# Two recurrent blocks in one launch: the layers of the first block in another order, one transpose used twice, four buffers for routed results, and longer runs at the end

## The chip, the cores and the metric

The kernel runs on one core of one Trainium2 chip. A core has five engines that run side by side, each through its own list of instructions in order: TensorE (PE; its weight loads are listed apart as PEld), VectorE (DVE), ScalarE (ACT), GpSimd (POOL) and SyncE (SP), which issues most of the transfers. Transfers run on 16 DMA engines. The metric is the device time of one execution in microseconds (us); lower is better.

## The reference, cut to what matters

The input is 32 sequences of 256 tokens, 128 numbers each (8192 tokens). There are two blocks of the form `x = x + s * silu(f)`, where `s` is a mixer and `f` a mixture of experts, both fed by the same layer norm of `x`.

```python
# block 0
xn = layernorm(x)
s = transformer(xn)          # 2 layers; layer 0 begins with layernorm(xn) * g + b
f = moe64(xn)                # 64 experts, top 8, 64 slots each, plus a shared expert
x = x + s * silu(f)
# block 1
xn = layernorm(x)
s = linear_attention(xn)
f = moe32(xn)                # 32 experts, top 1, plus a shared expert
x = x + s * silu(f)
```

What matters below: layer 0 of the transformer norms `xn`, which is a layer norm already. The second norm of a normed row is the same row times one number, the *ratio* of that token. So the router and the shared expert read `xn`, and the attention projection reads `xn` times the ratio of each token.

## The kernel before, in words

**Tiles.** Tokens are worked on in 16 groups of 512 (`g`), four tiles of 128 tokens each. Rows with a token on each partition are kept on the chip for the whole run (`s_rows`, also `s_all`). Matrix products need the other form, a channel on each partition, so rows are transposed on TensorE (four 128x128 transposes into one bank of `ps_tr`, of which there are two) and copied out by ScalarE. Groups go in pairs `p` = 0 to 7; a pair in one layer is a unit, so block 0's transformer has 16 units.

**Block 0.** In step `k` of a loop over units, `softmax` does the attention of unit `k`. Beside it `beside(k)` does the second norm, the first half (`widen`, L733) and second half (`narrow`, L748) of the feed-forward part of earlier units, and then `project` (L624, L634) for unit `k + 1`. The order of the units is written out by hand (`order_of`, L594): (0,0), (1,0), (2,0), (0,1), (3,0), (1,1), (4,0), (2,1) and so on, pair first, layer second. Layer 1 of a pair comes three or four units after its layer 0.

`enter(g)` loads `x`, takes its statistics on VectorE (L411, L412), and computes `xn` on POOL (L432); it stores `xn` to a table in DRAM, transposes it and keeps the transposed form `xs` (five buffers, `lent[g]`) for `choose` (router, L450) and `shared` (shared expert, L489 to L501). `norm_t(g)` makes the input of `project`. In layer 0 it takes `z` = `xn` * ratio on POOL (L608, four instructions), transposes it (L152, four) and copies it (L612) to `xt`; groups 0 and 1 have their `z` from `enter`. In layer 1, and for the feed-forward part, it norms `s_rows` first (L129 to L145).

In every second step `search` looks for the tokens of each expert on VectorE (L508, L509, 1024 elements wide), a quarter of the tokens at a time; each quarter ends with three fills of zeros in DRAM, together some 4.1 MB, issued by SP. When all quarters are found, `experts` gathers rows (L548), multiplies (L562, L574), scales the result into `e_y` (L584, ScalarE) and adds it to `sums` in DRAM with an indirect transfer issued by POOL (L585). `e_y` and `s_y`, the result of the shared expert (L500), share two buffers (tag "y").

**Block 1.** `route` (router, shared expert `shared1`, whose result goes to `back` in DRAM), `send` (scatters rows by expert), `linear_attention`, `routed` (expert tiles; results are added to `back` by an indirect transfer, L1070), and `finish`, which loads `back` (L1110), takes its silu (L1111, ScalarE), multiplies and adds (L1113, L1114, VectorE) and stores the output (L1115). A column of `s_rows`, `numbers`, says to which row of `back` each token's result goes. A group lies in `back` in the order of the tokens: on a partition stand two tokens that follow each other, and then two others, so a transfer has runs of 1 KB.

**Order.** The instructions are not run in the order of the program. `arrange` takes all of them, a cost for each and what each needs, and writes down one order for every engine (a list schedule, forward and backward passes). The loops above thus set what may run beside what, and `arrange` sets where each instruction stands. All buffers are a part of what it knows.

Of the kernel before, what the change touches and what calls it, by code (L numbers as in the profile page):

```python
# [18 lines left out]
F32 = mybir.dt.float32  # L19
# [8 lines left out]
P = 128  # L28
# [38 lines left out]
def recurrent_kernel(ctx: ExitStack, tc: tile.TileContext, x, consts, small0, wsd, wgu, wd, small1, bias1, wr, out):  # L67
# [24 lines left out]
    xslot = dram.tile([S1 * P, D + 2], F32, name="xslot")  # L92
    back = dram.tile([T + S1 * P, D], F32, name="back")

    def rows(ap, g):
        return ap[g * GW : (g + 1) * GW].rearrange("(b p j) d -> p b (j d)", p=P, j=2)

    def halves(ap, g):
        return ap[g * GW : (g + 1) * GW].rearrange("(b p j) d -> p b j d", p=P, j=2)

    def merged(tile_):
        return tile_.rearrange("p (b j) d -> p b (j d)", j=2)
# [1 line left out]

    s_rows = keep.tile([P, NT, D + 2], F32, name="s_rows")
    s_all = s_rows[:, :, :D]
    numbers = s_rows[:, :, D].rearrange("p (b j) -> p b j", j=2)
    pool.iota(numbers, [[SEQ, BATCH], [1, 2]], base=1, channel_multiplier=2, allow_small_or_imprecise_dtypes=True)
    cc, n_cc = columns(CONSTS)
    con = keep.tile([P, n_cc], F32, name="con")  # L110

# [154 lines left out]
    def shared1(g, inner=False):  # L266

        wk = works[0] if g < EARLY else work(g)
        xt = xt_at[g]
        hs = wk.tile([P, 2, GW], F32, tag="wide", name="f_h", bufs=1)  # L270
        for c in range(2):
            gp, up = bank("sc", 4), bank("sc", 4)
            pe.matmul(gp, par1("sg", c * P, P), xt, start=True, stop=True)
            pe.matmul(up, par1("su", c * P, P), xt, start=True, stop=True)
            if not inner and g < TANH:
                act.activation(hs[:, c], gp, AF.Tanh, scale=0.5)
                vec.scalar_tensor_tensor(hs[:, c], hs[:, c], 1.0, gp, ALU.add, ALU.mult)
            else:
                act.activation(hs[:, c], gp, AF.Silu)
            vec.tensor_tensor(hs[:, c], hs[:, c], up, ALU.mult)  # L280
            yield
        ps = bank()
        for j in range(GT):
            for c in range(2):
                pe.matmul(  # L285
                    ps[:, j * D : (j + 1) * D], hs[:, c, j * P : (j + 1) * P], par1("sd", c * D, D),
                    start=c == 0, stop=c == 1,
                )
        ys = wk.tile([P, GT, D], F32, tag="out", name="f_y")
        act.activation(ys, ps.rearrange("p (t d) -> p t d", d=D), AF.Copy, scale=0.5 if not inner and g < TANH else 1.0)  # L290
        sp.dma_start(rows(back, g), merged(ys))
        yield

    def run(*steps):
# [30 lines left out]
    with ExitStack() as c0:  # L325
# [72 lines left out]
        pool.iota(ciota, [[1, C0]], base=0, channel_multiplier=0, allow_small_or_imprecise_dtypes=True)  # L398
        cand = wf.tile([P, NG // 4, C0], F32, name="cand", bufs=1)
        keys, lent, found, twice = {}, {}, [], {}  # L400
        ratio = w0.tile([P, NG, GT], F32, name="ratio")

        def enter(g):

# [14 lines left out]
            if g < 2:  # L419
                for a, b in ((3, 4), (2, 5)):  # L420
                    pool.tensor_tensor(rs[:, a], rs[:, a - 2], power, ALU.pow)
                    vec.tensor_tensor(rs[:, b], mv[:, :, 0], rs[:, a], ALU.mult)
                twice[g] = wk.tile([P, GT, D], F32, name="z", bufs=4)
                for dst, a, b in ((twice[g], 3, 4), (xn, 2, 5)):
                    for j in range(GT):
                        vec.tensor_scalar(dst[:, j], xi[:, j], rs[:, a, j : j + 1], rs[:, b, j : j + 1], ALU.mult, ALU.subtract)
            else:
                pool.tensor_scalar(rs[:, 4], mv[:, :, 0], -1.0, 0.0, ALU.mult, ALU.add)
                pool.tensor_tensor(rs[:, 0], rs[:, 0], rs[:, 2], ALU.mult)
                pool.tensor_tensor(ratio[:, g], rs[:, 0], rs[:, 3], ALU.mult)  # L430
                for j in range(GT):
                    pool.tensor_scalar(xn[:, j], xi[:, j], rs[:, 4, j : j + 1], rs[:, 2, j : j + 1], ALU.add, ALU.mult)  # L432
            yield
# [51 lines left out]
        def shared(g):  # L485
# [10 lines left out]
            yp = bank()  # L496
            for j in range(GT):
                pe.matmul(yp[:, j * D : (j + 1) * D], hs[:, j * P : (j + 1) * P], sd, start=True, stop=True)
            ys = wk.tile([P, GT, D], F32, tag="y", name="s_y")
            act.copy(ys, yp.rearrange("p (t d) -> p t d", d=D))  # L500
            sp.dma_start(rows(moe0[0], g), merged(ys))  # L501
            yield
# [37 lines left out]
        def experts(q):  # L540
# [35 lines left out]
                    start=True, stop=True,  # L576
                )
            yield
            ye = wk.tile([P, 2, D], F32, tag="y", name="e_y")
            for h in range(2):  # L580
                for u in range(2):
                    at = slice(u * C0, (u + 1) * C0)
# [8 lines left out]

        order_of = [(0, 0), (1, 0), (2, 0), (0, 1)]  # L594
        for p in range(3, NG // 2):
            order_of += [(p, 0), (p - 2, 1)]
        order_of += [(p, 1) for p in range(NG // 2 - 2, NG // 2)]

        def norm_t(g, copy, again=True):

            xs = s_all[:, g * GT : (g + 1) * GT]
            z = twice.pop(g, None) if not again else None
            if z is None:
                z = wk.tile([P, GT, D], F32, name="z", bufs=4)
                if again:
                    normed(wk, xs, z)
                for j in range(0 if again else GT):
                    pool.tensor_scalar(z[:, j], xs[:, j], ratio[:, g, j : j + 1], 0.0, ALU.mult, ALU.add)  # L608
            yield
            ps = transposed(z)  # L610
            xt = wk.tile([P, GW], F32, tag="xt", name="xt", bufs=4)
# [494 lines left out]
    def finish(g):  # L1106

        tl = slice(g * GT, (g + 1) * GT)
        gr = xt_at[g].rearrange("p (t d) -> p t d", d=D)
        ins = sp.dma_start(merged(gr), rows(back, g))  # L1110
        act.activation(gr, gr, AF.Silu)  # L1111
        yield
        vec.tensor_tensor(gr, gr, s_all[:, tl], ALU.mult)  # L1113
# [379 lines left out]
```

## Time and profile before

| | |
|---|---|
| median of 3 runs | 1182.28 us (1179.81 to 1184.58) |
| profiled execution | 1182.8 us, of which its span is 1181.0 us |
| mean granted TensorE clock | 0.977 |
| busy: PE, PEld, DVE, ACT, POOL | 92%, 70%, 69%, 63%, 53% |
| DMA | 124.84 MB, mean 106 GB/s |

The span runs from the first to the last instruction; 1.8 us lie around it. In a row of the groups of instructions, the numbers after the count are the time in which any instruction of the group ran, the mean duration of one in ns, and the idle time of the engine just before them with what ended it. Matrix instructions overlap, so a mean duration is longer than the step from one to the next. In the trace a float32 product is two TensorE instructions, and a transpose is one. In the chain of work that ended last, each row has its start, its length and what ran.

### The profile page before, as it was taken

What the parts mean: (1) busy time and instruction counts of PE and PEld (TensorE: products, weight loads), DVE (VectorE), ACT (ScalarE), POOL (GpSimd) and SP (SyncE); (2) the same over time, 40 slices, a digit from 0 to 9 for tenths busy, and PEclk for the clock granted to TensorE, in tenths of its full rate; (3) what the DMA queues carried; (4) which work ended last, traced back from release to release, by engine and by line L of the source; (5) the groups of instructions that cost most, each with busy time, mean ns of one, the idle gap of its engine ahead of it and who ended that gap; (6) DMA issues with size and microseconds to landing.
All of it is one profiled execution on the core that took longest, in us unless ns stands there. A gap on an engine that the chain in (4) does not pass through costs nothing.

```text
span 1181.0 us, 21680 instructions
## 1 busy us (share of the span) xinstructions
PE 1092.3 (92%) x7207; PEld 822.1 (70%) x7207; DVE 818.6 (69%) x2599; ACT 744.5 (63%) x1717; POOL 627.4 (53%) x936
## 2 busy tenths in 40 slices
PE   6999999999999999999999997999999899999970
PEld 4657577576675676686677576667677799899870
DVE  6797579579579755355455669695767766766746
ACT  4776677577586677577586576464666565656633
POOL 6252734625612456746752638251677467667760
PEclk9999999999999999999999989999999899999995
DMA  6023302511411442232230215411322379888858
GB/s 215 18 63 111 106 24 60 178 29 40 173 31 65 135 108 52 56 85 56 50 64 5 50 45 172 122 64 45 135 73 67 90 192 236 203 204 226 210 89 286
DMA packets 110563, 124.84 MB, mean 106 GB/s; under 512 B 17296, under 2 KB 85488, under 8 KB 110448
## 3 DMA queue, kind: packets, MB, share of 16 engines
q1 hardware_dynamic: 90160, 108.40, 29.2%
q0 software_dynamic: 20288, 15.02, 8.8%
q8 instruction: 59, 0.97, 0.3%
q14 instruction: 56, 0.46, 0.1%
HBM read 75.54 MB, written 47.84 MB: 104 GB/s over the span
## 4 chain that ended last, share of the span: by engine, by line
PE 59%; DVE 16%; ACT 11%; DMA 6%; POOL 4%; issue 4%; SPq 1%; DVEq 0%; POOLq 0%; ACTq 0%
PE ps_mm L748 7%; PE ps_mm L733 7%; PE ps_sc L1055 5%; PE ps_tr L152 4%; PE ps_mm L698 4%; PE ps_mm L624 3%; PE ps_tr L685 3%; PE ps_sc L652 3%; PE ps_mm L1065 3%; ACT a_pr L667 2%; PE ps_mm L634 2%; PE ps_mm L285 2%; PE ps_tr L998 2%; PE ps_mm L562 2%; DVE key L509 2%
## 5 line engine op out<-in xcount | busy, mean ns | idle before, releaser
L1070 POOL DMA_INDIRECT back<-e_ys,e_toi x84 | 132.4, 1577 | 62.3 <-ACT e_ys L1069 46.2
L733 PE MATMUL ps_mm<-xt,sw 128*128 128x512 f32 x256 | 130.4, 613 | 4.0 <-ACT m_h L735 2.0
L667 ACT ACTIVATE a_pr<-ps_sc,a_nm 128x256 f32<-128x256 f32 x256 | 120.2, 486 | 18.1 <-DVE a_nm L658 17.6
L748 PE MATMUL ps_mm<-sw,m_h 128*128 128x128 f32 x1024 | 126.4, 277 | 4.1 <-ACT e_y L584 3.6
L748 PEld LDWEIGHTS ps_mm<-sw,m_h 128*128 128x128 f32 x1024 | 119.4, 192 | 8.8 <-ACT e_y L584 4.6
L735 ACT ACTIVATE m_h<-ps_mm,fold 128x512 f32<-128x512 f32 x128 | 86.7, 689 | 30.0 <-PE ps_mm L733 29.2
L658 DVE TENSOR_REDUCE a_nm<-ps_sc 128x2 f32<-128x512 f32 x128 | 82.6, 680 | 29.2 <-PE ps_sc L652 28.9
L131 POOL TENSOR_SCALAR bn_rs<-bn_mv 128x4 f32<-128x4 f32 x80 | 17.5, 219 | 158.6 <-DVE bn_mv L130 136.4
L585 POOL DMA_INDIRECT sums<-e_y,sidx x32 | 51.8, 1619 | 76.4 <-ACT e_y L584 53.3
L145 POOL TENSOR_SCALAR z<-s_rows,bn_rs 128x128 f32<-128x128 f32 x192 | 89.5, 528 | 4.1
L1055 PE MATMUL ps_sc<-e_xt,e_w 128*128 128x128 f32 x672 | 90.6, 279 | 1.1 <-ACT e_xt L1093 1.1
L686 ACT COPY a_pt<-ps_tr 128x512 f32<-128x512 f32 x128 | 73.0, 597 | 28.9 <-PE ps_tr L685 26.4
L939 POOL DMA_INDIRECT xslot<-s_rows,dest x64 | 66.5, 1039 | 45.4 <-DVE hot L930 27.3
L1055 PEld LDWEIGHTS ps_sc<-e_xt,e_w 128*128 128x128 f32 x672 | 84.4, 195 | 5.3 <-issue 2.4
L132 POOL TENSOR_TENSOR bn_rs<-bn_rs,power 128x4 f32<-128x4 f32 x80 | 86.2, 1077 | 0.5
L716 DVE TENSOR_TENSOR s_rows<-ps_mm,s_rows 128x512 f32<-128x512 f32 x32 | 22.0, 688 | 83.8 <-PE ps_mm L711 83.8
L685 PE MATMUL ps_tr<-con,a_pr 128*128 128x128 f32 x512 | 75.7, 279 | 0.4 <-DVE a_pr L676 0.4
L652 PE MATMUL ps_sc<-a_qk,a_qk 64*128 64x256 f32 x512 | 74.1, 404 | 2.1 <-ACT a_pr L667 1.8
L685 PEld LDWEIGHTS ps_tr<-con,a_pr 128*128 128x128 f32 x512 | 60.0, 144 | 20.3 <-issue 14.0
L470 POOL TENSOR_TENSOR r_wt<-sel,r_ex 128x256 f32<-128x256 f32 x16 | 11.7, 732 | 106.8 <-DVE r_su L466 47.3
L1058 DVE TENSOR_TENSOR e_hs<-e_hs,ps_sc 128x256 f32<-128x256 f32 x84 | 34.3, 412 | 44.9 <-ACT e_hs L1057 44.6
L733 PEld LDWEIGHTS ps_mm<-xt,sw 128*128 128x128 f32 x256 | 40.2, 190 | 36.1 <-ACT m_h L735 15.7
(258 smaller groups left out, 2867.9 us busy)
## 6 DMA issues: line engine op xcount, KB each, us to landing
e_w<-in_wr_dram SPq DMA_DIRECT2D x84, 384.0 KB, 4.5
xslot<-zero SPq DMA_DIRECT2D x4, 1560.0 KB, 9.2
e_wg<-in_wgu_dram SPq DMA_DIRECT2D x16, 384.0 KB, 3.3
back<-zero SPq DMA_DIRECT2D x4, 1536.0 KB, 12.6
e_x<-xslot SPq DMA_DIRECT2D x21, 260.0 KB, 4.2
x_in<-in_x_dram SPq DMA_DIRECT2D x16, 256.0 KB, 3.0
tab<-s_rows SPq DMA_DIRECT2D x32, 128.0 KB, 2.1
sums<-s_y SPq DMA_DIRECT2D x16, 256.0 KB, 2.1
```

Of the source, the lines that this page charges most:

```text
L132: pool.tensor_tensor(rs[:, 0], rs[:, 0], power, ALU.pow)
L145: ins = pool.tensor_scalar(dst[:, j], src[:, j], rs[:, 1, j : j + 1], rs[:, 0, j : j + 1], ALU.add, ALU.mult)
L652: pe.matmul(sc[h][:, j * SEQ : (j + 1) * SEQ], qk[0][hd, q0 : q0 + P], qk[1][hd, b * SEQ : (b + 1) * SEQ], start=True, stop=True,)
L658: vec.tensor_reduce(nm[:, 2 * h : 2 * h + 2], sc[h].rearrange("p (j k) -> p j k", k=SEQ), AX.X, ALU.max, negate=True)
L667: act.activation(pr[:, n], sc[h][:, j * SEQ : (j + 1) * SEQ], AF.Exp, bias=nm[:, n : n + 1], accum_out=su[:, n : n + 1],)
L685: pe.transpose(pts[:, n * P : (n + 1) * P], pr[:, n, k * P : (k + 1) * P], ident)
L686: act.copy(pt[k], pts.rearrange("p (h q) -> p h q", q=SEQ))
L733: pe.matmul(ps, par("w1", l * FF0 + f * P, P), xt, start=True, stop=True)
L735: act.activation(h, ps, AF.Silu, scale=GELU, bias=fold[:, l, 3 + f : 4 + f])
L748: pe.matmul(ps[:, j * D : (j + 1) * D], hs[f][:, j * P : (j + 1) * P], par("w2", l * FF0 + f * D, D), start=f == 0, stop=f == 3,)
L1055: pe.matmul(ps[:, c * P : (c + 1) * P], wt[:, c * P : (c + 1) * P], xt, start=True, stop=True)
L1070: ins = pool.indirect_dma_start(out=back, out_offset=bass.IndirectOffsetOnAxis(ap=to, axis=0), in_=ys, in_offset=None, compute_op=ALU.add,)
```

## The change

1. **Layer order.** All eight units of layer 0 come first, then all eight of layer 1.
2. **One transpose for two uses.** From group 4 on, `enter` writes the ratio of the 512 tokens to DRAM (four columns of 128 numbers, so 512 runs of 4 bytes) and reads it back as one row of 2 KB onto every partition; both transfers are issued by SP. `norm_t` of layer 0 then multiplies the transposed `xs` by it in one VectorE instruction, with no `z`, transpose or copy. Groups 2 and 3 get their `z` in `enter` from `x` (POOL).
3. **Four buffers for `e_y`.** `e_y` has its own four buffers; `s_y` is written over `xs`, which is free then.
4. **2 KB runs.** A group in `back` has four rows to a partition (`broad`), and `numbers` is counted accordingly; so the store of the shared expert and the load in `finish` have runs of 2 KB. The output keeps its order.

```diff
+    ratios = dram.tile([NG, GW], F32, name="ratios")
+
+    def broad(ap, g):
+        return ap[g * GW : (g + 1) * GW].rearrange("(p t) d -> p (t d)", t=GT)
...
-    numbers = s_rows[:, :, D].rearrange("p (b j) -> p b j", j=2)
-    pool.iota(numbers, [[SEQ, BATCH], [1, 2]], base=1, channel_multiplier=2, allow_small_or_imprecise_dtypes=True)
+    numbers = s_rows[:, :, D].rearrange("p (g t) -> p g t", t=GT)
+    pool.iota(numbers, [[GW, NG], [1, GT]], base=1, channel_multiplier=GT, allow_small_or_imprecise_dtypes=True)
...
-        sp.dma_start(rows(back, g), merged(ys))
+        sp.dma_start(broad(back, g), ys.rearrange("p t d -> p (t d)"))
...
-                pool.tensor_tensor(ratio[:, g], rs[:, 0], rs[:, 3], ALU.mult)
+                pool.tensor_tensor(rs[:, 5], rs[:, 0], rs[:, 3], ALU.mult)
+                if g < 4:
+                    twice[g] = wk.tile([P, GT, D], F32, name="z", bufs=4)
+                    for j in range(GT):
+                        pool.tensor_scalar(twice[g][:, j], xi[:, j], rs[:, 4, j : j + 1], rs[:, 3, j : j + 1], ALU.add, ALU.mult)
+                else:
+                    sp.dma_start(ratios[g].rearrange("(t p) -> p t", p=P), rs[:, 5])
+                    twice[g] = wk.tile([P, GW], F32, tag="z", name="ratio", bufs=4)
+                    sp.dma_start(twice[g], ratios[g : g + 1].broadcast_to([P, GW]))
...
-            ys = wk.tile([P, GT, D], F32, tag="y", name="s_y")
+            ys = xt.rearrange("p (t d) -> p t d", d=D)
...
-            ye = wk.tile([P, 2, D], F32, tag="y", name="e_y")
+            ye = wk.tile([P, 2, D], F32, name="e_y", bufs=4)
...
-        order_of = [(0, 0), (1, 0), (2, 0), (0, 1)]
-        for p in range(3, NG // 2):
-            order_of += [(p, 0), (p - 2, 1)]
-        order_of += [(p, 1) for p in range(NG // 2 - 2, NG // 2)]
+        order_of = [(p, l) for l in range(LAYERS) for p in range(NG // 2)]
...
-            xs = s_all[:, g * GT : (g + 1) * GT]
             z = twice.pop(g, None) if not again else None
+            if g >= 4 and z is not None:
+                xt = wk.tile([P, GW], F32, tag="xt", name="xt", bufs=4)
+                vec.tensor_tensor(xt, lent[g], z, ALU.mult)
+                yield xt
+                return
             if z is None:
                 z = wk.tile([P, GT, D], F32, name="z", bufs=4)
-                if again:
-                    normed(wk, xs, z)
-                for j in range(0 if again else GT):
-                    pool.tensor_scalar(z[:, j], xs[:, j], ratio[:, g, j : j + 1], 0.0, ALU.mult, ALU.add)
+                normed(wk, s_all[:, g * GT : (g + 1) * GT], z)
...
-        ins = sp.dma_start(merged(gr), rows(back, g))
+        ins = sp.dma_start(xt_at[g], broad(back, g))
```

The hunks stand in the order of the file: the head of the kernel, `shared1`, `enter`, `shared`, `experts`, `order_of`, `norm_t`, `finish`.

More of the change, by code (lines that the diff above doesn't have):

```diff
@@ L400, in recurrent_kernel @@
         keys, lent, found, twice = {}, {}, [], {}
-        ratio = w0.tile([P, NG, GT], F32, name="ratio")
         def enter(g):
```

## The prediction

> **What bounds the kernel now.** I read the page first, then busy time by stage, the waits of TensorE, the costliest groups, and the last 30 us. About 0.5% (5.9 us) is what a measurement here can tell from no change. The busy times by stage (us; busy us and count of each engine, clock, DMA share, GB/s):
>
> ```profile
> core 0: us, PE busy (x) PEld busy (x) DVE busy (x) ACT busy (x) POOL busy (x), PEclk, DMA share, GB/s
> 22.00:412.00 390.00, 377.65 (x2347) 256.21 (x2346) 309.17 (x1034) 271.76 (x691) 171.88 (x379) 1.00 0.24 78
> 412.00:664.00 252.00, 245.86 (x1788) 179.76 (x1788) 126.63 (x397) 171.58 (x438) 146.98 (x216) 1.00 0.28 60
> ...
> 1130.00:1181.00 51.00, 16.95 (x124) 15.41 (x122) 29.30 (x67) 16.48 (x32) 14.24 (x14) 0.68 0.68 191
> ```
>
> The stages are: layers with search (to 412), layers with experts (to 664), and the end. TensorE is busy 97% and 98% of the first two: it is the bound, and what other engines lose there counts only where TensorE comes to wait. Only in the last stage is it mostly idle. The waits of TensorE, longest first, show how little is left there:
>
> ```profile
> PE ps_mm L498 <- DVE s_h L494: 4.7, 7, 0.9
> ...
> PE ps_mm L748 <- ACT e_y L584: 3.6, 5, 1.2
> ...
> PE ps_tr L152 <- POOL z L145: 1.6, 2, 1.4
> ...
> PE ps_mm L733 <- ACT e_y L584: 1.3, 4, 0.7
> ```
>
> So this change is worth what it takes off TensorE, and not much more. The groups it touches:
>
> ```profile
> L152 PE MATMUL ps_tr<-con,z 128*128 128x128 f32 x256 | 47.2, 284 | 2.9 <-POOL z L145 1.6 <-ACT a_pt L686 0.7
> ...
> L612 ACT COPY xt<-ps_tr 128x512 f32<-128x512 f32 x64 | 37.6, 589 | 17.4 <-PE ps_tr L152 17.0
> ...
> L432 POOL TENSOR_SCALAR s_rows<-x_in,bn_two 128x128 f32<-128x128 f32 x56 | 24.3, 447 | 0.2
> ...
> L608 POOL TENSOR_SCALAR z<-s_rows,ratio 128x128 f32<-128x128 f32 x56 | 19.7, 370 | 0.2
> ```
>
> A mean of 284 ns is not the price of a transpose, since the next one starts before it ends. The chain of waits shows the step, 0.44 us for four:
>
> ```profile
> 443.89 0.44 PE ps_tr L152 x4
> ```
>
> **One transpose for two uses.** Twelve groups lose four transposes each: 48 x 0.11 = 5.3 us of TensorE, in a stage where TensorE is 97% busy. With the waits before them (2.9 us for 256, so 0.5 for 48) I take 5.8. The upper end is the whole group's time, (47.2 + 2.9) / 256 x 48 = 9.4; the lower end is nothing, if TensorE waits instead. ScalarE loses 12 x 0.589 = 7.1 us and POOL 56 x 0.370 - 8 x 0.447 = 17.1 us. Both hide under TensorE (271.8 and 171.9 us busy of 390), so I count nothing for them.
>
> VectorE gains 12 multiplications of 512 columns, 0.68 us each by the rows of the end (L1113, below): 8.2 us. It is busy 309 of 390 us, so on average they fit, but in the steps with a search it has no room (rival one).
>
> SP gains 24 transfers. An issue of `x_in`, 256 runs, takes SP 0.41 us, so I take 0.8 for 512 runs and 0.4 for the read: 14 us in 390 us, hidden while nothing on SP is urgent. The read waits for the write to land, and what stands behind it on SP (the next write, loads of `x`, stores to the table) waits too. The landing times of the nearest transfers:
>
> ```profile
> back<-zero SPq DMA_DIRECT2D x4, 1536.0 KB, 12.6
> ...
> x_in<-in_x_dram SPq DMA_DIRECT2D x16, 256.0 KB, 3.0
> ...
> tab<-r_wt SPq DMA_DIRECT2D x32, 64.0 KB, 2.0
> ...
> bias<-in_bias_dram SPq DMA_DIRECT2D x1, 320.0 KB, 5.3
> ```
>
> The shortest runs here, 256 bytes (`tab<-r_wt`), landed in 2.0 us; the only row spread to all partitions (`bias`) took 5.3 us for 320 KB and an ordinary load of the same 256 KB took 3.0. I take 2.1 and 3.0, so 5 us for the round trip, and 5.3 for a leg as the worse end. The Trainium skill speaks against this write: "DMA: Bandwidth & Descriptors", Specifications, says that below 512 bytes a transfer is done as read-modify-write, and these runs have 4. It gives no price for runs of 4 bytes, and no row of this trace shows data in runs that short.
>
> What covers the round trip: in the built order of VectorE, the multiplications of groups 6 to 15 stand at least 20 us of VectorE work behind the statistics of their group. Groups 4 and 5 have the least. Their statistics run at 61.9 us before, POOL has the ratio of group 4 some 3 us later (one power at 1.64 us and four short steps at 0.2 to 0.25), and the multiplication stands behind the fifth step of the first quarter's search, which began at 80.3 and ended at 81.5. On SP the order is write 4, read 4, write 5, read 5, the third behind the wait of the second: 65 + 2 x 2.1 + 3.0 + 2.4 for four issues = 74.6 us, 7 us early. Groups 8, 10, 11, 14 and 15 have their writes behind fills (12.6 us to land, 17.7 with the round trip) and at least 15 us of VectorE work before their use, which at its 79% share of this stage is 19 us. Cost: none.
>
> **Layer order.** The work of a unit stays. What moves is on VectorE and POOL. Steps 4 and 6 (with search) project layer 0 and no longer layer 1: eight statistics and eight aggregates less (272 and 161 ns, 3.5 us), 1.4 us for two multiplications more, so 2.1 us lighter. Step 2 takes over an `enter` (3.5 us) for a norm and is 1.4 us heavier. Between -2.8 us and nothing on the path; I take nothing, as only 4.7 us of waits (L498) hang there. Later, steps 9 and 11 prepare layer 1 in place of layer 0: on POOL two full norms, 2 x (0.22 + 1.08 + 0.25 + 4 x 0.53) = 7.3 us in place of 3.0. POOL is busy 58% of that stage, and steps 10 and 12 have that load already: from first score to first score, step 10 takes 43.9 us (459.0 to 502.9) and step 12 43.8, no more than step 11 with its 43.8. Cost: none; without that cover 2 x 4.3 = 8.6 us.
>
> **Four buffers for `e_y`.** ScalarE waits for a landing of `sums` in the first step with experts:
>
> ```profile
> 435.61 4.50 DMA sums<-e_y,sidx
> ...
> 440.26 0.36 ACT e_y L584
> ```
>
> TensorE then waits 0.7 us at 441.8. The other waits for `e_y` (0.6 us in each step) end with ScalarE's own four instructions, which stay. Gain: 0.7 us, at most the 4.9 of both rows.
>
> **2 KB runs.** The loads of `back` stand at the end:
>
> ```profile
> L1113 DVE TENSOR_TENSOR xt<-xt,s_rows 128x512 f32<-128x512 f32 x16 | 10.5, 683 | 3.4 <-ACT xt L1111 3.4
> L1114 DVE TENSOR_TENSOR xt<-xt,x 128x512 f32<-128x512 f32 x16 | 10.3, 682 | 0.0
> L1111 ACT ACTIVATE xt<-xt 128x512 f32<-128x512 f32 x16 | 10.1, 630 | 8.2 <-DMA xt<-back 6.9
> ```
>
> VectorE sets the pace: 20.8 us for 16 groups, 1.3 each, while ScalarE follows the loads at 0.73 each (13 in 9.47 us in the timeline). So runs can win only what VectorE waits for the first loads, 3.4 us at most; I take 1.0, as the first landing (3.0 us after its issue) is mostly latency. The Trainium skill's "Perfetto Trace Analysis", DMA Optimizations, counts transfers under 2 KB as paying much overhead each and longer ones as the main remedy where DMA is the limit. By it the gain could reach the whole 3.4; the row says that DMA is not the limit behind the first few loads.
>
> **Sum.** 5.8 + 0.7 + 1.0 = 7.5 us. The profiled execution has 1182.8 us (span 1181.0), 0.5 above the median of the runs: 1182.8 - 7.5 = 1175.3, and against the median 1174.8. I say 1175.
>
> **Rivals.**
> *More than the transposes.* The upper ends hold: 9.4 + 4.9 + 3.4 = 17.7 us, 1165. For it: the two search steps get lighter as well. Against it: TensorE idles only 3% there. 12%, 1163 to 1170.
>
> *Given back on VectorE.* The multiplications sit in the path of `project`, where POOL, TensorE and ScalarE worked before; VectorE runs through each search almost without a gap (the waits for `s_h` are TensorE's largest here). If each of the 12 is on the path, 8.2 us come back: 1182.8 - 7.5 + 8.2 = 1183.5; by half, 1179. 18%, 1178 to 1185.
>
> *Slower: the round trip of groups 4 and 5.* With a landing time L for each leg, the multiplication of group 5 can start at 65 + 3 L + 2.4. It stands at 81.5 in VectorE's order with everything behind it, the score maxima among them, so each us past that is lost by all engines: it decides from L = 4.7 us. At 5.3 (the `bias` row) it costs 1.8 us; at 9.2 (the 1560 KB fill of `xslot`) 13.5, which makes 1189; at 12.6, 23.7, which makes 1199. For it: 4-byte runs have no row here. Against it: 2 KB in 512 runs is little beside these fills. 15%, 1187 to 1199.
>
> That the change does not do what it says is hardly open: the built program has 48 transposes and 12 copies less.
>
> **How the numbers follow.** Forecast 55%, 1170 to 1180; the three rivals 12, 18 and 15%. Faster by over 0.5% means under 1176.4: of the forecast 42 in 55, and the first rival, 54%. Slower means over 1188.2: nearly all of the last, 15%. The rest, 31%, is the same. The range 1166 to 1188 leaves out some 6% below and 14% above.
>
> **What would show it.** Right: L152 on `z` has 208 transposes and TensorE's busy time falls by about 5 us, all of it before 412 us, with the first score of unit 9 some 5 us earlier; the end from the first load of `back` is about 1 us shorter. Wrong: a TensorE or VectorE wait that ends with the ratio's transfer near 80 us (last rival); waits of L624 for the multiplication spread over the first 400 us (second rival); a stage after 664 us that changes its length, which no step here foresees.

## The result and the profile after

The changed kernel takes 1195.99 us (median of 4 runs, 1192.42 to 1196.96) against 1182.87 us for the kernel before on the same chip: a ratio of 1.0106, 95% interval 1.008 to 1.0132. The prediction said 1175 us, 1166 to 1188. It was wrong in sign: the change costs 13 us. The profiled execution has 1192.42 us, span 1190.5, mean granted clock 0.975.

Busy time by stage, as it was read before (us; busy us and count of each engine, clock, DMA share, GB/s):

```profile
core 0: us, PE busy (x) PEld busy (x) DVE busy (x) ACT busy (x) POOL busy (x), PEclk, DMA share, GB/s
22.00:412.00 390.00, 362.91 (x2240) 244.76 (x2237) 299.44 (x961) 255.75 (x667) 142.68 (x306) 0.98 0.36 84
412.00:664.00 252.00, 246.32 (x1778) 179.42 (x1778) 139.62 (x465) 171.88 (x440) 156.55 (x230) 1.00 0.27 60
```

In the first stage TensorE was busy 377.65 us and is now busy 362.91, VectorE, ScalarE and POOL were busy less too, and the layers with search are unfinished at 412 us: so somebody waits. The waits of TensorE name the place. Columns: us in total, number of waits, longest:

```profile
PE ps_mm L634 <- DVE s_rows L726: 12.9, 2, 8.9
...
PE ps_mm L758 <- ACT e_y L596: 3.6, 5, 1.2
...
PE ps_mm L743 <- ACT e_y L596: 0.8, 4, 0.2
```

Two waits of `project` (L634, L624 before) for VectorE make 12.9 us, which is the size of the whole loss. VectorE's rows say why VectorE was late (start, length, line, operation, and in brackets the idle time before and its releaser):

```profile
79.14 1.23 DVE L520 MAX8 cand<-key 128x8 f32<-128x1024 f32 x1
84.57 0.69 DVE L613 TENSOR_TENSOR xt<-xs,ratio 128x512 f32<-128x512 f32 x1 [4.20 <-DMA ratio<-ratios]
85.18 0.08 DVE L521 MATCH_VALUE_LOAD key<-cand,key 128x8 f32 x1
85.25 1.21 DVE L521 MATCH_REPLACE8 key<-cand,key 128x1024 f32<-128x1024 f32 x1
86.37 0.68 DVE L726 TENSOR_TENSOR s_rows<-ps_mm,s_rows 128x512 f32<-128x512 f32 x1
95.57 0.69 DVE L613 TENSOR_TENSOR xt<-xs,ratio 128x512 f32<-128x512 f32 x1 [8.52 <-DMA ratio<-ratios]
```

L613 is the new multiplication, for groups 4 and 5. VectorE had been through its search step, came to the multiplication, and stood 4.20 and 8.52 us for the ratio. The residual add (L726) has its place in the queue behind it. TensorE waits for that add: the add reads a bank of `ps_mm`, and L634 writes one. Who kept the ratio is seen in SP's queue (issues only):

```profile
70.39 0.36 SPq L440 DMA_DIRECT2D ratios<-bn_two  x1
72.42 0.52 SPq L447 DMA_DIRECT2D tab<-s_rows  x1
78.97 0.33 SPq L442 DMA_DIRECT2D ratio<-ratios  x1
79.39 0.39 SPq L440 DMA_DIRECT2D ratios<-bn_two  x1
...
91.77 0.34 SPq L442 DMA_DIRECT2D ratio<-ratios  x1
```

The write of group 4 (L440) is issued at 70.39, and the read behind it (L442), which waits for the landing, at 78.97: 8.6 us. Only then comes the write of group 5, and its read 12.4 us later. In the chain of work that ended last, the landing of that second write is one piece of 12 us:

```profile
79.39 12.31 DMA ratios<-bn_two
91.77 3.71 DMA ratio<-ratios
95.57 0.69 DVE xt L613
```

The loss thus lies between the first score of unit 1 and that of unit 2, at 48.1 and 103.6 us:

```profile
48.10:103.60 55.50, 40.18 (x219) 24.15 (x217) 39.84 (x127) 28.94 (x77) 19.01 (x43) 0.88 0.26 43
103.60:472.00 368.40, 356.10 (x2229) 241.74 (x2228) 276.29 (x896) 243.79 (x615) 153.33 (x306) 1.00 0.38 93
```

The second stretch ends with the first score of unit 10. The same two before:

```profile
48.90:90.50 41.60, 38.44 (x224) 24.20 (x222) 39.79 (x125) 30.38 (x79) 21.42 (x51) 1.00 0.15 45
90.50:459.00 368.50, 358.06 (x2275) 245.97 (x2274) 272.60 (x902) 250.09 (x624) 170.55 (x354) 1.00 0.27 86
```

So 13.9 us are lost in one place, and from there to unit 10 nothing is lost and nothing is won. From unit 10 to the end this execution, the fastest of its four, takes 718.5 us where it was 722.0; so its span is only 9.5 us longer. Of these 3.5 us, 1.6 lie behind the first load of `back` (below); the rest is not explained.

The groups that the change touches, and the end:

```profile
L157 PE MATMUL ps_tr<-con,z 128*128 128x128 f32 x208 | 38.4, 283 | 3.5 <-POOL z L150 1.8 <-ACT a_pt L696 1.2 <-POOL r_wt L482 0.4
L622 ACT COPY xt<-ps_tr 128x512 f32<-128x512 f32 x52 | 30.6, 593 | 7.9 <-PE ps_tr L157 7.2
...
L613 DVE TENSOR_TENSOR xt<-xs,ratio 128x512 f32<-128x512 f32 x12 | 8.1, 685 | 17.3 <-DMA ratio<-ratios 12.7 <-ACT xs L450 4.6
...
L1121 ACT ACTIVATE xt<-xt 128x512 f32<-128x512 f32 x16 | 10.1, 630 | 6.1 <-DMA xt<-back 5.6
L1123 DVE TENSOR_TENSOR xt<-xt,s_rows 128x512 f32<-128x512 f32 x16 | 10.4, 683 | 2.5 <-ACT xt L1121 2.5
```

The transposes are 208, the multiplications cost 8.1 us as priced, and of their 17.3 us of idle time 12.7 end with the ratio's transfer. At the end VectorE waits 2.5 us for the silu where it waited 3.4; from the first load of `back` to the last instruction it is 27.3 us where it was 28.9.

### The profile page after: what moved, and what is told of

It is laid out like the page before. It is cut to its first block, busy times and chain, and to the rows that moved or that the text cites. A ratio compares the mean times of both kernels' runs of the same rounds, so it can differ in the third digit from the quotient of the medians.

```text
span 1190.5 us, 21588 instructions
## 1 busy us (share of the span) xinstructions
PE 1090.4 (92%) x7159; PEld 816.7 (69%) x7159; DVE 824.8 (69%) x2611; ACT 737.2 (62%) x1705; POOL 616.3 (52%) x888
## 4 chain that ended last, share of the span: by engine, by line
PE 62%; DVE 18%; ACT 9%; DMA 5%; issue 3%; POOL 2%; DVEq 0%; SPq 0%; ACTq 0%; POOLq 0%
PE ps_mm L758 8%; PE ps_mm L743 7%; PE ps_sc L1065 5%; PE ps_mm L634 5%; PE ps_mm L708 4%; PE ps_tr L695 4%; PE ps_tr L157 3%; PE ps_sc L662 3%; PE ps_mm L1075 2%; PE ps_mm L644 2%; DVE a_nm L668 2%; PE ps_mm L290 2%; PE ps_mm L574 2%; PE ps_mm L721 2%; PE ps_sc L982 2%
## 5 line engine op out<-in xcount | busy, mean ns | idle before, releaser
L743 PE MATMUL ps_mm<-xt,sw 128*128 128x512 f32 x256 | 130.8, 615 | 4.7 <-ACT m_h L745 2.2
L758 PE MATMUL ps_mm<-sw,m_h 128*128 128x128 f32 x1024 | 124.2, 276 | 3.9 <-ACT e_y L596 3.6
L758 PEld LDWEIGHTS ps_mm<-sw,m_h 128*128 128x128 f32 x1024 | 118.2, 191 | 8.2 <-ACT e_y L596 4.6
L150 POOL TENSOR_SCALAR z<-s_rows,bn_rs 128x128 f32<-128x128 f32 x192 | 92.0, 530 | 4.1
L949 POOL DMA_INDIRECT xslot<-s_rows,dest x64 | 66.1, 1032 | 45.3 <-DVE hot L940 27.3
L634 PE MATMUL ps_mm<-xt,sw 128*128 128x512 f32 x128 | 67.8, 651 | 13.7 <-DVE s_rows L726 12.9
L726 DVE TENSOR_TENSOR s_rows<-ps_mm,s_rows 128x512 f32<-128x512 f32 x32 | 22.0, 687 | 75.7 <-PE ps_mm L721 75.7
L743 PEld LDWEIGHTS ps_mm<-xt,sw 128*128 128x128 f32 x256 | 40.1, 189 | 39.4 <-ACT m_h L745 15.3
```

The costliest lines, as they stand in the source:

```text
L150: ins = pool.tensor_scalar(dst[:, j], src[:, j], rs[:, 1, j : j + 1], rs[:, 0, j : j + 1], ALU.add, ALU.mult)
L634: pe.matmul(ps, w[i], xt, start=True, stop=True)
L743: pe.matmul(ps, par("w1", l * FF0 + f * P, P), xt, start=True, stop=True)
L758: pe.matmul(ps[:, j * D : (j + 1) * D], hs[f][:, j * P : (j + 1) * P], par("w2", l * FF0 + f * D, D), start=f == 0, stop=f == 3,)
```

## The experiments

Two things had to be explained: the 13 us, and why 48 transposes fewer do not show after unit 2. Ratios are to the kernel before on the same chip; 95% intervals are in brackets. On two of the chips the kernel before takes 1215 and 1218 us. Two kernels with the new layer order show where the extra lies: on the chip with 1215 us the one with the order alone begins its `send` at 830.7 us, and on a chip with 1184 us the one with the 2 KB runs as well begins it at 832.6, while the ends are 1208.9 and 1180.2. So the stage studied here is the same, and whole times are compared in us only on one chip.

### What takes the 13 us

Theory A: the late round trip of groups 4 and 5, in one place. Theory B: the layer order, with small losses everywhere. Theory C: the short writes slow all other transfers. First, no trip at all, with `z` of all groups from 2 on made by POOL in `enter` and the transposes back:

```diff
-                if g < 4:
+                if g < 16:
-            if g >= 4 and z is not None:
+            if g >= 16 and z is not None:
```

> All groups from 2 on get z in enter on POOL, so there is no ratio transfer and the 48 transposes are back; layer order, four e_y buffers and 2 KB runs stay. Theory A (the changed kernel loses its time in one place, where groups 4 and 5 wait for the ratio): the wait of 12.9 us is gone and so are the 5.8 us saved on TensorE, which leaves the small gains, so 1181 us against 1183 before (0.998), and the first score of unit 2 at 90 us instead of 103.6. Theory B (the layer order costs some 5 us of scattered waits by itself): 1187 (1.003). Theory C (the 4-byte writes slow all other transfers and the scattered waits come from them): 1181, as A.

Second, the trip only from group 6 on (6 in place of 4 in the same two lines):

> Only groups 4 and 5 go back to z from POOL, the ratio transfer begins at group 6. Theory A: the wait of 12.9 us and the slower products just behind it (TensorE at a lower clock, some 2 us) are gone, and 8 transposes (0.9 us) are back: 1196 - 14.9 + 0.9 = 1182 us; if the rest of the saved transposes counts in full, it comes below the kernel before by 4.5 to 6 us, 1177. Theory B or C (some 5 us are lost elsewhere): 1182, that is the same as before although TensorE has 40 transposes less.

Third, the trip for all 12 groups, but with the write as 128 runs of 16 bytes (a partition's four numbers side by side); the multiplication then reads the ratio with a stride of four:

```diff
-                    sp.dma_start(ratios[g].rearrange("(t p) -> p t", p=P), rs[:, 5])
+                    sp.dma_start(ratios[g].rearrange("(p t) -> p t", t=GT), rs[:, 5])
...
-                vec.tensor_tensor(xt, lent[g], z, ALU.mult)
+                vec.tensor_tensor(
+                    xt.rearrange("c (t p) -> c t p", p=P), lent[g].rearrange("c (t p) -> c t p", p=P),
+                    z.rearrange("c (p t) -> c t p", t=GT), ALU.mult,
+                )
```

> The ratio is written as 128 runs of 16 bytes in place of 512 of 4, and the multiplication reads it with a step of 4. If the landing time goes with the number of short writes (8.5 to 12.3 us for 512), it falls to 3 to 4 us, the multiplication of group 5 stands ready by 80 us and the wait goes from 12.9 to under 2 us: 1182 to 1184 us by theory B (order costs 5 us), 1176 to 1178 by theories A and C (all transposes saved, no jam). If a short write costs the same however long it is alone, landing stays near 9 us and the time near 1195.

Fourth, the kernel before with the layer order alone:

> The kernel before with the layer order alone. Theory A and C: 1183 us, within 0.3% of before (forecast of the layer order: between 2.8 us less and nothing). Theory B: 1188 (1.004 to 1.005), with scattered waits in the first 400 us.

Measured: no trip 0.9979 (0.995 to 1.0007), from group six 1.0001 (0.9972 to 1.0029), 16-byte runs 0.9983 (0.9956 to 1.001), order alone 0.9967 (0.9938 to 0.9997). Three different ways of taking away the late pair each take away the whole loss, and the layer order costs nothing: A, and not B. The 16-byte runs had been expected at 0.994 to 0.996 under A, though, and miss that. The first score of unit 2 stands at 87.7, 88.3 and 90.0 us, not 103.6. SP's queue with 16-byte runs answers the one above:

```profile
70.25 0.33 SPq L440 DMA_DIRECT2D ratios<-bn_two  x1
72.28 0.52 SPq L447 DMA_DIRECT2D tab<-s_rows  x1
72.90 0.55 SPq L442 DMA_DIRECT2D ratio<-ratios  x1
73.54 0.41 SPq L440 DMA_DIRECT2D ratios<-bn_two  x1
...
77.58 0.33 SPq L442 DMA_DIRECT2D ratio<-ratios  x1
```

The same 2 KB from the same tile, issued at the same time, lets its read go 2.65 us later instead of 8.6, and the second 4.0 instead of 12.4. But these kernels are level with the kernel before; the transposes are 40 or 48 fewer in two of them, and the 5 us are not there. That is the second question below. The changed kernel again, on the chip of the next runs:

> The changed kernel again, beside the others on this chip, where the kernel before takes 1215 us. Theory A (two late multiplications, of groups 4 and 5, behind round trips of 12 us and more): the loss of 13 us stands here too, ratio 1.008 to 1.013, with the first score of unit 2 about 14 us later than in the run with 128 runs of 16 bytes. If the loss belonged to the first chip, the ratio would be 0.996 to 1.002, as in the runs without the late pair.

Measured: 1195.13 us against 1183.59 (and not 1215) for the kernel before on this chip, 1.0111 (1.0088 to 1.0133), with the first score of unit 2 at 104.6 us. The loss is not the first chip's.

Then the late write, but with the multiplication on GpSimd (`pool.tensor_tensor` in L613):

> The changed kernel with its write of 512 runs of 4 bytes as it is, and the multiplication on GpSimd. It tells what a late transfer costs when VectorE's queue does not stand behind it. If the 13 us come from what is queued behind the waiting multiplication on VectorE, most of them go: 0.994 to 0.997. If TensorE needs the product of group 5 itself by then, the loss stays, since the read still lands at 95 us: 1.005 to 1.010.

Measured: 0.9981 (0.9957 to 1.0006), beside 0.9907 for the same with 16-byte runs. In this build the scheduler also put the write of group 5 ahead of group 4's read, so not only the engine differs. TensorE now waits for the multiplication itself:

```profile
82.00 1.16 PE L721 MATMUL ps_mm<-sw,a_at 128*128 128x128 f32 x8
88.11 5.65 PE L634 MATMUL ps_mm<-xt,sw 128*128 128x512 f32 x8 [4.96 <-POOL xt L613]
```

That is 5 us in place of 12.9. Unit 1 to unit 2 takes 45.6 us, between the 55.5 of the changed kernel and the 39.3 of the 16-byte runs beside it. So the result lies between the two expectations: a late ratio costs some 6 us by itself (8.7 by the medians of the two kernels), and the rest came from two queues, VectorE's behind the waiting multiplication and SP's behind the waiting read. No run separates these two. The rows of the changed kernel give an estimate: the multiplications ended at 85.26 and 96.26 and TensorE began at 87.11 and 97.77, so VectorE's queue has at most 1.9 and 1.5 us; the write of group 5 went at 79.39 where it goes at 73.15 here, so SP's queue has some 6.

### What makes the write land late

The landing was measured by itself, in the kernel without the trip: four forms of write in turn over groups 4 to 15, each read back into a small tile that nothing uses.

```diff
+  512 x 4 B side by side:  short[g, :GW].rearrange("(t p) -> p t", p=P)  <- rs[:, 5]
+  512 x 4 B, 64 B apart:   short[g].rearrange("(t p s) -> p t s", p=P, s=16)[:, :, 0]  <- rs[:, 5]
+  128 x 16 B:              short[g, :GW].rearrange("(p t) -> p t", t=GT)  <- rs[:, 5]
+  128 x 4 B:               short[g, :P].rearrange("(p t) -> p t", t=1)  <- rs[:, 5, :1]
```

> The run without the trip, with a write and a read back added that nothing else uses, to measure the landing by itself: four forms of write in turn, three of each over groups 4 to 15: 512 runs of 4 bytes side by side; 512 runs of 4 bytes, 64 bytes apart; 128 runs of 16 bytes; 128 runs of 4 bytes. The time from the issue of the write to that of the read behind it is the landing (an upper bound where a transfer of rows stands between). If the number of runs sets it: both forms of 512 take 8 us and more, both forms of 128 under 5. If the shortness of a run sets it: the 128 runs of 4 bytes take 8 us too. If neighbours in one 64-byte line hinder each other: the spread 512 land in under 5 us.

Measured from the issue of a write to the issue of the read behind it, which waits for the landing. Each form came three times in the one profiled execution. SP's queue in the first round (writes L438, L441, L444, L447 in the order of the list above, their reads L439, L442, L445, L448):

```profile
79.33 0.56 SPq L438 DMA_DIRECT2D short<-bn_two  x1
80.02 0.43 SPq L441 DMA_DIRECT2D short<-bn_two  x1
89.76 0.33 SPq L439 DMA_DIRECT2D back<-short  x1
90.62 0.78 SPq L442 DMA_DIRECT2D back<-short  x1
...
104.79 0.42 SPq L444 DMA_DIRECT2D short<-bn_two  x1
105.30 0.38 SPq L447 DMA_DIRECT2D short<-bn_two  x1
...
108.81 0.32 SPq L445 DMA_DIRECT2D back<-short  x1
113.38 0.32 SPq L448 DMA_DIRECT2D back<-short  x1
```

Over the three rounds: 512 runs side by side 10.4, 9.1 and 10.6 us; 512 runs 64 bytes apart 10.6, 11.2 and 10.5; 128 runs of 16 bytes 4.0, 11.3 and 6.9; 128 runs of 4 bytes 8.1, 11.7 and 9.6. These are upper bounds where another transfer stands between, but before the reads at 8.1 and 11.3 us SP had issued nothing for 4 us, so there the landing itself was so late. The number of runs alone thus does not set it: by it the 128 runs of 4 bytes should have landed in under 5 us, and they did so in no round; their 8 us and more are what had been expected if the shortness of a run sets it. Neighbours in one line fall, since the spread form is no earlier. But shortness is not shown either: the 128 runs of 4 bytes always stood half a microsecond behind those of 16 bytes, and these too were late in two rounds of three, beside other transfers. In the whole kernels the 16-byte form landed in 2.4 to 5.0 us with GpSimd's multiplication, where the profile has the landing, but once in 13.0 in the kernel with a spare multiplication (below).

Two rows of the kernel before set limits to both explanations: `e_x<-xslot` loads 512 runs of 520 bytes in 4.2 us, and `tab<-r_wt` writes 256 runs of 256 bytes in 2.0. What the late writes wait for is not the moving of data: from 82 to 87 us, with the first two writes still out, the DMA engines' share of busy time is 0.00. So it is measured that 16-byte runs land earlier where it matters, 2.65 and 4.0 us against 8.6 and 12.4; whether their number or their length does it stays open.

### Where the transposes' gain went

Theory V: the 12 multiplications fill VectorE's queue. Theory S: the order of the work gives back what TensorE saves, whatever one does. Three kernels ran with the changed kernel's second run. The 16-byte form with its multiplication on GpSimd:

```diff
-                vec.tensor_tensor(
+                pool.tensor_tensor(
```

> The run with 128 runs of 16 bytes, but with the multiplication on GpSimd in place of VectorE. Its question is where the 5.3 us go that the transposes free on TensorE in the main loop. Theory V (VectorE's queue: the 12 multiplications of 1.1 us delay what stands behind them): with them off VectorE the 5.3 us come out, 0.998 - 5.3/1215 = 0.9935 to 0.995. Theory S (the order of the work: other engines' results come at their own times, and TensorE waits for them that much longer): 0.997 to 0.999, with the loss of TensorE in the main loop still near 59 us. Should GpSimd be too late with it (some 1.3 us each, behind its other steps), 1.000 or above.

The changed kernel with no ratio at all (the second norm of groups 4 to 15 in layer 0 is left out), ScalarE copying in its place:

```diff
-                    (write and read of the ratio)
+                    twice[g] = lent
...
-                vec.tensor_tensor(xt, lent[g], z, ALU.mult)
+                act.copy(xt, lent[g])
```

> The changed kernel without the ratio's write, read and multiplication: ScalarE copies the transposed first-norm rows into the attention's tile, so the second norm of groups 4 to 15 in layer 0 is left out. Against the run with all of z made on GpSimd this takes away the 48 transposes and GpSimd's z, and adds nothing. Theory V: 5.3 us less than that run, 0.9935 or lower. Theory S: as that run, 0.997 to 0.999, with TensorE's own work 5.3 us smaller and its waits that much longer. It is the bound on what the transposes can be worth in this order.

The kernel before with the layer order and the 2 KB runs alone:

> The kernel before with the layer order and the 2 KB runs alone. If the two add, 0.9967 - 1.0/1215 = 0.996 (the prediction's term for the runs is 1.0 us, and the changed kernel's stretch from the first load of the routed sums to the end was 1.6 us shorter). If the runs bring nothing, 0.9967. Above 0.998 the layer order's gain in the first call was noise.

Measured: GpSimd's multiplication 1176.33 us, 0.9939 (0.9914 to 0.9965); no ratio 1179.26, 0.9969 (0.9953 to 0.9986); order and runs 1183.62, 1.0002 (0.9985 to 1.0018). The kernel with no ratio stands at the edge of what S had said, the one with GpSimd's multiplication where V had put it, and the layer order's gain alone was noise. So the gain is to be had, and S, as a bound on the order, falls: the same four parts with a faster write and another engine stand 18.8 us below the changed kernel and 7.3 below the kernel before. TensorE's rows, in the 16-byte form with GpSimd's multiplication, where the changed kernel has its two long waits:

```profile
83.19 1.02 PE L637 MATMUL ps_mm<-xt,sw 128*128 128x512 f32 x2
84.61 3.07 PE L637 MATMUL ps_mm<-xt,sw 128*128 128x512 f32 x6 [0.40 <-POOL xt L613]
```

One wait of 0.40 us is left. The same comparison on one chip:

> The changed kernel with all of z made on GpSimd (no ratio transfer, the 48 transposes back), beside the three others on one chip. With theories A and V both true it stands where the transposes are still paid and nothing waits: about 5 us above the 16-byte run with GpSimd's multiplication, level with the 16-byte run with VectorE's, ratio 0.997 to 0.9995.

> The changed kernel with the ratio written as 128 runs of 16 bytes, multiplication on VectorE. Theories A and V: 12 to 15 us below the changed kernel, and level with the run without the trip (0.997 to 0.9995), since VectorE's 12 multiplications give the 5.3 us back. If the 5 us between the two earlier calls was the chips' difference and not VectorE's queue, it lies level with the GpSimd run.

> 16-byte runs and GpSimd's multiplication again, beside the others: 0.992 to 0.9965, and 4 to 7 us below the 16-byte run with VectorE's multiplication. It holds all four parts of the change and should stand where the prediction had put the changed kernel.

Measured: no trip 1214.33, 0.998 (0.9953 to 1.0006); 16-byte runs with VectorE's multiplication 1215.8, 0.9997 (0.9968 to 1.0025); with GpSimd's 1205.34, 0.9907 (0.9877 to 0.9938). The 10.5 us between the last two are more than the 4 to 7 expected, though the intervals, each some 3 us to either side, reach down to 5.

Is it VectorE's time? A multiplication of the same size whose result nobody reads was put on VectorE beside GpSimd's, and, since room had to be made for it, `e_y` got two buffers in both kernels of the pair:

```diff
+                spare = wk.tile([P, GW], F32, name="spare", bufs=1)
+                vec.tensor_tensor(spare, lent[g], lent[g], ALU.mult)
...
-            ye = wk.tile([P, 2, D], F32, name="e_y", bufs=4)
+            ye = wk.tile([P, 2, D], F32, name="e_y", bufs=2)
```

> The 16-byte run with GpSimd's multiplication, and on VectorE a multiplication of the same size put beside it whose result nobody reads (8.3 us in all; the routed results' buffers are two, to make room, as in the run beside it). Theory V (VectorE's time in its queue): 3 to 6 us above the run beside it. If the 16-byte run lost by the stride of its operand and by TensorE's waiting for that result, and not by VectorE's occupation: 0 to 1.5 us.

> The 16-byte run with GpSimd's multiplication, with the routed results of block 0 in two buffers of their own in place of four. The prediction gave the four buffers 0.7 us: 0.9907 to 0.9939 as with four, and up to 0.0006 more. Beyond 0.997 the buffers would carry part of the gain.

Measured: 1176.75 us with the spare multiplication, 0.9956 (0.9939 to 0.9974), and 1176.91 without, 0.9947 (0.9929 to 0.9964). Twelve more VectorE instructions of 0.69 us cost nothing that can be measured where nothing waits for their results, and theory V as I had put it falls too. Left are theory Q, that TensorE waits for a result that has its place in VectorE's queue, and theory T, that the 16-byte form's strided operand (1.13 us for 0.69) costs the time. So: no transfer, no stride, the tile multiplied by itself (again without the second norm of groups 4 to 15), once on VectorE and once on GpSimd, beside the strided form.

```diff
-                act.copy(xt, lent[g])
+                vec.tensor_tensor(xt, lent[g], lent[g], ALU.mult)     (or pool.tensor_tensor)
```

> The changed kernel without the ratio's transfer: the multiplication stays on VectorE, at its full size and without stride (0.69 us), but multiplies the tile by itself, so that the second norm of groups 4 to 15 is left out. Theory Q (TensorE's product waits for a result that stands in VectorE's queue, whatever the stride): 4 to 9 us above the same on GpSimd, 0.997 to 1.000. Theory T (the stride of the 16-byte form's operand, 1.12 for 0.69 us, is what gave the 5 us back): level with the same on GpSimd, 0.992 to 0.996.

> The same without the transfer, with the multiplication on GpSimd. Both theories: 0.992 to 0.996, as the 16-byte run with GpSimd's multiplication; if it lies 2 us or more below that run's 0.9907 to 0.9947, the transfer itself still costs something there.

> The 16-byte run with VectorE's multiplication again, on the chip of the two others. Theory Q: within 2 us of the plain multiplication on VectorE. Theory T: 4 us or more above it.

Measured: on VectorE 1180.18 us, 0.9973 (0.9956 to 0.9989); on GpSimd 1176.99, 0.994 (0.9918 to 0.9963); strided on VectorE 1182.4, 0.999 (0.9973 to 1.0006). VectorE against GpSimd is 3.2 us without any stride, less than the 4 to 9 that Q had said, and the two intervals overlap. The further 2.2 us of the strided form, stride and transfer together, lie within what the intervals leave open; Q had said under 2 and T 4 or more, so neither is met. GpSimd's form with the transfer (0.9939 and 0.9907, on other chips) and without it (0.994) are level within their intervals, so no cost of the mended round trip shows there. VectorE's rows of the plain form have a place of the kind that Q means:

```profile
81.94 0.69 DVE L611 TENSOR_TENSOR xt<-xs 128x512 f32<-128x512 f32 x1
82.55 0.48 DVE L134 BATCH_NORM_STATS2 bn_st<-s_rows 128x6 f32<-128x128 f32 x2
82.95 0.18 DVE L135 BATCH_NORM_AGGREGATE bn_mv<-bn_st 128x2 f32<-128x6 f32 x1
83.04 0.45 DVE L134 BATCH_NORM_STATS2 bn_st<-s_rows 128x6 f32<-128x128 f32 x2
83.41 0.67 DVE L724 TENSOR_TENSOR s_rows<-ps_mm,s_rows 128x512 f32<-128x512 f32 x1
```

The multiplication feeds TensorE, and so does the residual add (L724); with both on one engine the add comes last, and TensorE waits 0.90 us for it at 84.1. With the multiplication on GpSimd it waits 0.41 us for the same add. The windows of the two, unit 1 to unit 2 and unit 2 to unit 10, on VectorE first and on GpSimd second:

```profile
47.30:88.60 41.30, 37.78 (x219) 23.35 (x217) 39.61 (x128) 28.91 (x77) 18.79 (x43) 1.00 0.16 45
88.60:456.90 368.30, 357.29 (x2231) 243.22 (x2230) 276.07 (x896) 243.30 (x615) 154.99 (x306) 1.00 0.27 86
```

```profile
48.00:87.30 39.30, 36.47 (x206) 22.04 (x204) 37.58 (x115) 30.07 (x77) 17.76 (x38) 1.00 0.17 48
87.30:454.20 366.90, 356.13 (x2240) 242.10 (x2239) 271.29 (x896) 243.13 (x614) 163.63 (x323) 1.00 0.27 86
```

This splits the loss. Against GpSimd's plain form, VectorE's costs 2.0 us in the first stretch and 1.4 in the second. But of these 3.4 us only 0.9 are idle time of TensorE; 2.5 are its busy time (395.07 against 392.60 in the rows above, for nearly as many instructions), and the scheduler gave each kernel an order of its own on every engine. That GpSimd is the better place is measured; that Q is the reason is not shown. Against VectorE's plain form, the changed kernel has the same multiplications and the trip on top: 55.5 - 41.3 = 14.2 us in the first stretch (57.7 - 41.3 = 16.4 in its second run), and 368.4 against 368.3 in the second. The last pair also speaks against theory C: the ten later trips load the DMA engines more (a share of 0.38 against 0.27) and cost no time.

## Why the prediction was wrong, step by step

**The round trip was mis-sized, and this decided the sign.** The step that failed is its "Cost: none". The prediction had priced the write at 2.1 us from the row of 256-byte runs (`tab<-r_wt`), and had the ratio of group 5 on the chip at 74.6 us, "7 us early". It came at 95.57. Of the 21 us, the two landings are 6.5 and 10.2 (8.6 and 12.3 for 2.1), the start is 5.4 (70.4 for 65, since POOL began the ratio of group 4 only at 66.5), the read is 0.7 (3.7 for 3.0); some 2 us go off, since the issues, counted apart, lie within the measured legs. The place was right: the plain form, which waits for no transfer, multiplies group 5 at 81.94, where the prediction had 81.5. So was the order on SP, write 4, read 4, write 5, read 5. From the later start the trip decides from 70.4 + 3 L + 2.4 = 81.5, that is L = 2.9 us and no longer 4.7, so little cover was left even for ordinary landings. In the 16-byte form with GpSimd's multiplication, with those landings of 2.4 to 5.0 us and write 5 ahead of read 4, no multiplication waited for the ratio: all their waits end with `xs`.

The third rival was what happened, at 1187 to 1199. It had one landing time for all three legs; measured were 8.6 and 12.3 us for the writes and 3.7 for the read. It had been given 15% because 2 KB looked small beside the fills. Bytes were the wrong measure: the row taken as nearest had 256 runs of 256 bytes, and the write had 512 of 4. Which of these two differences made it late stays open; neither 2.1 nor the worse end of 5.3 bounded it.

The Trainium skill bears on this in "Perfetto Trace Analysis", DMA Instruction — HWDGE (DVE, Sync): the last descriptor raises the semaphore only once the write before it is confirmed, which it says can take surprisingly long when the target is HBM. This agrees with writes that land 9 us after their issue while the DMA engines move nothing, and the prediction did not weigh it. The read-modify-write below 512 bytes, which it did weigh, does not tell the late writes from the others here: runs of 256 bytes landed in 2.0 us, and runs of 16 in 2.4 to 5.0 in the form with GpSimd's multiplication, and all of these are under 512.

**The transposes: gone, but the forecast gain came only with the multiplication on GpSimd.** TensorE does shed them: 208 are left. From the first score of unit 1 to that of unit 10 it is busy 392.75 us in the 16-byte form with GpSimd's multiplication, against 396.68 with order and runs alone; these 3.9 us stand for the 5.3 that the prediction took from its rows, and the stretch is 4.1 us shorter. By the medians of the whole runs the two are 7.3 us apart, 1176.33 against 1183.62, of which `e_y` may have a part. With the multiplication on VectorE, 3.2 us are given back, by the plain forms. The second rival had foreseen a loss there, of up to 8.2 us, with the multiplications themselves in the path; part of it came, on top of the third rival, and its mechanism is not shown. "On average they fit" was true of VectorE's time, as the spare multiplication showed. ScalarE is no free place either: the copies of the kernel with no ratio stand at 0.9969, between the others.

**Layer order: right at nothing.** 0.9967 (0.9938 to 0.9997) alone, and 1.0002 (0.9985 to 1.0018) with the 2 KB runs.

**Four buffers for `e_y`: the wait went, but its 0.7 us do not show in the time.** ScalarE no longer stands for the landing of `sums`. TensorE's waits at L758 are 3.6 us as before, as the prediction had said of them. Those at L743 fell from 1.3 us, the longest 0.7, to 0.8, the longest 0.2; with two buffers of its own beside GpSimd's multiplication they are 1.6, the longest 0.7, and with four 0.9, the longest 0.2. The whole times, 0.9947 (0.9929 to 0.9964) with two and 0.9939 (0.9914 to 0.9965) with four on another chip, can't be told apart.

**2 KB runs: of the right size, as far as one can see.** 1.0 us was forecast; the stretch from the first load of `back` is 1.6 us shorter in the changed kernel, and 0.6 between the order alone (28.3 us) and the order with the runs (27.7), which ran on different chips. VectorE's wait fell by 0.9. The whole times do not resolve it.

**The sum.** Its 7.5 us are near what the 16-byte form with GpSimd's multiplication measures: 1176.33 us where the prediction said 1175, 7.3 us below the kernel before on that chip and 12.2 on another. That is another kernel than the one forecast, its transposes show 3.9 us for 5.3, and the rest of the gain is not placed, so the nearness is in part luck. This version beats both kernels. The changed kernel differs from the sum by the two terms that were counted as hidden: some 14 to 16 us for the trip and some 3 for VectorE.

## What to carry to other kernels

A small transfer can't be priced by its bytes when its runs are far shorter than those of every row at hand: take the bound that hurts, measure the landing, and look at what stands in the queues behind both the wait for the landing and the wait for the data. An operation that moves to an engine with time to spare is not free by that alone: try the other engines too, also one on which it takes longer.

## What the runs showed of the hardware that was not expected

After TensorE's two waits the granted clock fell, so that a wait cost more than its length. The clock stands behind POOL's busy time, in stretches of the changed kernel around the waits:

```profile
82.00:87.00 5.00, 1.16 (x9) 0.97 (x8) 2.43 (x4) 0.59 (x1) 0.00 (x0) 1.00 1.06 142
87.00:89.00 2.00, 1.73 (x2) 0.30 (x2) 0.05 (x1) 0.00 (x0) 0.00 (x0) 0.62 0.93 24
89.00:97.70 8.70, 0.00 (x0) 0.00 (x0) 2.13 (x8) 0.00 (x0) 0.00 (x0) 0.50 0.57 109
97.70:102.30 4.60, 4.53 (x8) 1.83 (x8) 3.33 (x15) 0.00 (x0) 3.08 (x7) 0.63 0.00 0
```

The clock is 0.62 after the first wait, 0.50 in the second, and still 0.63 in the 4.6 us after it. The six products that follow the wait (L634) took 4.50 us, and the same six in the 16-byte form with GpSimd's multiplication, at clock 1.00, took 3.07. The Trainium skill's "TensorE: Matmul & The Clock Gate", What's actually happening, has this as a gate that halves the clock after an idle window of some 3.4 us and opens again after as long a busy one; the rows, with waits of 3.95 and 8.93 us before these products, agree.

A write of 2 KB can take as long to land as the fills of 1.5 MB did before (12.6 us for `back`): 8.6 and 12.4 us for the two that mattered, with 512 runs of 4 bytes. As 128 runs of 16 bytes it let its read go after 2.65 and 4.0 us at the same place, and took up to 13.0 elsewhere. And GpSimd, which takes 1.27 us for the multiplication that VectorE does in 0.69 (1.54 and 1.13 with the strided operand; 1.04 and 0.69 for the tile by itself), is the better place for it here, by 3.2 us in the plain forms.
